# A two-layer graph network on one core: last products tile by tile, nine buffers for adj, the branch's verdict earlier among the products, four blocks by parts

## The chip, the cores and the metric

One core of a Trainium2 chip runs the whole kernel. A core has TensorE (PE, matrix products, with a queue of its own, PEld, for loading weights), VectorE (DVE), ScalarE (ACT), GpSimd (POOL) and SyncE (SP), each with an instruction queue that is worked through in order, 16 DMA engines, on-chip memory and PSUM, in which TensorE accumulates. SP, ACT and POOL issue the DMAs here. The metric is the device time of one execution in microseconds; less is better.

## The reference, cut to what matters

x is 4096 x 512 and adj 4096 x 4096, both float32. adj is nonzero in under one per cent of its entries (two random draws of 1/256, made symmetric, and the diagonal).

```python
def layer0(inp, adj, W, b):
    rowsum = adj.sum(axis=1)
    d = where(rowsum > 0, rowsum ** -0.5, 0.0)
    return relu(((d[:, None] * adj * d[None, :]) @ inp) @ W + b)

def layer1(inp, adj, W, a, wtrans):
    h = inp @ W
    e = leaky_relu(h @ a[:512] + (h @ a[512:]).T, 0.2)
    att = softmax(where(adj > 0, e, -1e12), axis=1)
    neg = -softmax(where(adj > 0, -e, -1e12), axis=1)
    return elu(concatenate([att @ inp, neg @ inp], axis=1) @ wtrans)

h = relu(layernorm(x));  x = x + layer0(h, adj, ...)
h = relu(layernorm(x));  x = x + layer1(h, adj, ...)
```

## The kernel before, in words

**Layer 0** is a dense product. It is computed as d * (adj @ y) + b with y = d * (relu(LN(x)) @ W), y staying on chip as 32 row blocks of 128 x 512. The 32 row blocks of the output are done in eight groups, `GROUPS`: (first block, count) = (26,6), (16,4), (20,4), (0,4), (4,4), (8,4), (12,4), (24,2). For a group, PSUM holds one accumulator of 128 x 512 for each of its blocks, and the inner loop runs over the 32 blocks j of y: a tile `at` of the transposed adj is loaded by SP (`load_at`, L794; two blocks j a tile in groups of four, four in the last group) and each accumulator gets one product a block (`multiply`, L804). A product of 128 x 512 float32 is two TensorE instructions.

*Group 0* (L817 to L859) also makes y. For each block j: POOL loads x (`load_x`, five buffers), DVE takes its statistics (L410), ACT normalizes it to hx (L633), PE transposes it (L645), DVE copies it, PE multiplies it by W (`project`, L676); SP loads the row block of adj in four pieces of 512 KB (`load_adj`, L657, pool `ain`, four buffers), three of them summed by ACT (L666) and one by DVE (L668), the sum becomes d (`scale`, L688 to L693), and ACT scales the projection to y (L699). Then six products follow with that block.

*Groups 1 to 7* are `group` (L907). It begins with `finish0` for the group before (L734): DVE takes all accumulators from PSUM (L741), then for each block POOL loads x, DVE adds it, takes the layer norm's statistics, ACT normalizes to h (L633), DVE makes the two scores of the attention (L757), and h with its score goes out as rows to eight tables in memory (`put_row`, L420): the table of the early pair by POOL, the seven others by ACT, or, for group 6, kept in a list `puts` and issued by SP at the end of group 7. Group 6's scores s reach other rows by `spread_s` (PE and ACT, through memory) and `load_s` (a broadcast load). DVE also packs each at tile into a byte mask (`pack`, L711, with flags at L715), which POOL stores into the tables' rows (L727). While groups 2, 3 and 4 run, the at tiles of groups 7, 6 and 5 are loaded once more, through the pool `early` with two buffers, and packed ahead of time (`EARLY`, L921). The pool `at` of groups 1 to 6 has five buffers.

*Lists.* From the flags DVE makes sorted lists of neighbours (`make_lists`, rounds at L375 and L377, spread over the steps of groups 3 to 6), which POOL turns into row indices (L390).

*The turn to layer 1.* A pair is two blocks of 64 rows. The pair 16 (blocks 33 and 32) is done early, inside and behind group 7: POOL gathers its rows of table 4 (`gather0`), DVE and ACT make the weights (`weights0`), PE multiplies (`product0`, L997) once group 7's products are done. `finish0` of blocks 24 and 25 follows, then `judge` (L880), which decides on DVE with one tiny product (`ok_ps`, L902) whether the lists hold everything: its `verdict` is read by all engines and chooses a branch, sparse or dense (L1181). Here it is sparse.

**Layer 1**, `sparse_layer1` (L1054), goes through the other 31 pairs from 17 on. A pair takes 22 gathers on POOL (8, 6 and 8 of 128 rows each, L428), in six tile slots, two pairs deep; the even block needs the first two parts, the odd block the last two. For a block: scores (L440), exponentials (L453), masks (L460), a tree of sums (L465 to L471) giving `total`, 14 products u (L1110), a column sum of total on PE (cs, L476) and its inverse (L478), us = u scaled (L1119), its transposes (tp, L486) and, for a pair, eight products with wtrans (o, L1133), elu and the output. The blocks in `first` (the first two) have exponentials part by part as gathers come, and their column sum behind the products u; the others have the column sum ahead of them. wtrans (`wt_sb`, 2 MB) is loaded by POOL behind the gathers of the first pair (L1156). In pairs 18 to 22, a copy on POOL (`mark`, L1078) waits for the last gather of its pair.

The scheduler may move instructions within an engine's queue unless `keep_in_program_order` pins one. A pool that opens gets memory that a closed one has left, and its first loads wait for the last users of that memory.

Of the kernel before, what the change touches and what calls it, by code (L numbers as in the profile page):

```python
# [19 lines left out]
P = 128  # L20
# [12 lines left out]
NE = 8  # L33
# [224 lines left out]
def gcn_gat_kernel(  # L258
# [97 lines left out]
    def rows_of(g, e):  # L356
        return table[g][e * ER : e * ER + EN, :].rearrange("(k p) c -> p k c", p=P)
# [21 lines left out]
    def table_rows(g, c, lst):  # L379

        li = list_pool.tile([P, CAPS[c]], I32, tag=f"li{c}", name=f"li{g}_{c}")
# [111 lines left out]
    with sbuf(name="y0", bufs=1) as y_pool, sbuf(name="wa", bufs=1) as wa_pool, sbuf(name="bits", bufs=2) as bits_pool, sbuf(name="small0", bufs=4) as small, ExitStack() as lists:  # L493
# [14 lines left out]
        )  # L508
        dummy = list_pool.tile([P, sum(CAPS)], F32, tag="lst", name="dummy")
        dummy = dummy[:, : NH * STR // P].bitcast(I32)  # L510
        nc.gpsimd.memset(dummy, EN)
        for g in range(2):
            nc.gpsimd.dma_start(
                out=lst_dram[g].rearrange("(p n) o -> p (n o)", p=P), in_=dummy
            )
        flags = [list_pool.tile([P, EJ * NE, 2 * NH], F32, name=f"flags{g}") for g in range(2)]
# [3 lines left out]
        wa_bc = [wa_pool.tile([P, F], F32, tag=f"wa{g}", name=f"wa{g}") for g in range(2)]  # L520
        zero = list_pool.tile([P, 3 * EN], F32, tag="keys", name="zero")
        zero = zero[:, :ROW].bitcast(I32)
        nc.gpsimd.memset(zero, 0)
        for g in range(NTAB):
            nc.gpsimd.dma_start(
                out=table[g].rearrange("(e r) c -> e r c", r=ER)[:, EN, :], in_=zero[:NE]
            )

        nc.gpsimd.dma_start(
            out=rows_of(tab0, late0 // EJ)[:, late0 % EJ : late0 % EJ + n_late, :],  # L530
            in_=zero.unsqueeze(1).to_broadcast([P, n_late, ROW]),
        )
        y_tiles = {}
# [5 lines left out]
        def make_keys(g):  # L539


            bits = list_pool.tile([P, 2, EJ * NE, NH], BF16, tag="flag16", name=f"flag16_{g}")
# [11 lines left out]
            keys[g] = list_pool.tile([P, 3, EN], F32, tag="keys", name=f"keys{g}")  # L554
            lst[g] = list_pool.tile([P, sum(CAPS)], F32, tag="lst", name=f"lst{g}")
# [6 lines left out]
            one = list_pool.tile([P, EN], F32, tag="one", name=f"one{g}")  # L562
            for c in range(3):
                nc.vector.tensor_scalar(one, key[:, c], 0.0, None, ALU.is_gt)
                nc.vector.tensor_reduce(cnt[:, c : c + 1], one, AX.X, ALU.add)

        def make_places(g):
# [3 lines left out]
            for e in range(NE + 1):  # L571
                nc.tensor.matmul(o_ps[:, e, 0:3], before[:, e, :], cnt, start=True, stop=True)
            o = list_pool.tile([NH, NE, 3], F32, tag="o", name=f"o{g}")
            tot = list_pool.tile([NH, 4], F32, tag="tot", name=f"tot{g}")
            nc.vector.tensor_copy(tot[:, 0:3], o_ps[:, NE, 0:3])
            begin = list_pool.tile([NH, 3], F32, tag="begin", name=f"begin{g}")
            nc.vector.memset(begin[:, 0:1], 0.0)
# [156 lines left out]
        def finish0(work, i0, acc, last=False):  # L734

            to_last = (i0, len(acc)) == GROUPS[-2]
            ys = []
            n_y = 4 if (i0, len(acc)) in GROUPS[-2:] else 6
            for j, a in enumerate(acc, i0):
                y = work.tile([P, F], F32, tag="y", name=f"y{j}", bufs=n_y)  # L740
                nc.vector.scalar_tensor_tensor(  # L741
                    y, a, d_all[:, j : j + 1], b_bc, ALU.mult, ALU.add
                )
                ys.append(y)
            for j, y in enumerate(ys, i0):
                xt = work.tile([P, F], F32, tag="xr", name=f"xr{j}")
# [36 lines left out]
        def load_s(queue, i0, n):  # L783

            j = i0
            while j < i0 + n:
                k = min(i0 + n, j - j % 4 + 4) - j
                queue.dma_start(
                    out=s_bc[j // 4][:, j % 4 * P : (j % 4 + k) * P],
                    in_=s_dram[j * P : (j + k) * P].partition_broadcast(P),  # L790
                )
                j += k

        def load_at(pool, i0, n, j0, nj):  # L794
# [8 lines left out]

        def multiply(acc, j0, at, between=None):  # L804
            for c in range(at.shape[1]):
                for it, a in enumerate(acc):
                    if between and it == len(acc) // 2:
                        between()
                    nc.tensor.matmul(  # L809
                        a,  # L810
                        at[:, c, it * P : (it + 1) * P],
                        y0[j0 + c],
                        start=j0 + c == 0,
                        stop=j0 + c == NJ - 1,
                    )

        i0, n = GROUPS[0]  # L817
        with sbuf(name="w0", bufs=1) as w0_pool, sbuf(name="at6", bufs=5) as at_pool, sbuf(name="ain", bufs=4) as ain, sbuf(name="ln", bufs=3) as ln_pool:
            w0_sb = w0_pool.tile([P, FC, F], F32, name="w0_sb")
# [60 lines left out]
        def judge():  # L880
# [20 lines left out]
            ok_ps = bank("ok_ps")  # L901
            nc.tensor.matmul(ok_ps[0:1, 0:1], all_ok, ones[:, 0:1], start=True, stop=True)  # L902
            verdict = const.tile([1, 1], I32, name="verdict")
# [3 lines left out]
        def group(b, work, at_pool, early, step):  # L907

            nonlocal pending
            i0, n = GROUPS[b]  # L910
            nj = 8 // n
            for jp in range(NJ // 2):
                if jp == 0:
                    finish0(work, *pending)
                    acc = [bank(f"acc{i0 + k}") for k in range(n)]
                if 2 * jp % nj == 0:
                    at = load_at(at_pool, i0, n, 2 * jp, nj)
                    multiply(acc, 2 * jp, at)
                if (i0, n) not in EARLY:
# [4 lines left out]
                if jp == 8:  # L924
                    spread_s(pending[0], len(pending[1]))
                if jp == 12:
                    load_s(nc.scalar, pending[0], len(pending[1]))
                step(jp)
            pending = (i0, acc)

        late = ctx.enter_context(sbuf(name="late", bufs=1, side="right"))
        late_h = late.tile([P, n_late, ROW_W], F32, name="late_h")
        late_m = late.tile([P, EJ, TT * P], U8, name="late_m")
        ut0 = late.tile([P, 2, FC, P], F32, name="ut0")

        with sbuf(name="work0", bufs=2) as work, sbuf(name="at", bufs=5) as at_pool, sbuf(name="early", bufs=2) as early:
            for b in range(1, len(GROUPS) - 1):
# [14 lines left out]
        with sbuf(name="work2", bufs=2) as work, sbuf(name="at2", bufs=5) as at_pool, sbuf(name="scratch", bufs=1) as scratch, sbuf(name="pair", bufs=1) as pair:  # L952
# [39 lines left out]

            def product0(r):
                u0[r] = bank(f"u{r}")
                for gt, k0, n in parts0(r):
                    for k in range(n):
                        nc.tensor.matmul(  # L997
                            u0[r],
# [3 lines left out]
                            stop=False,  # L1002
                        )

            def late_product0(r):
# [13 lines left out]
            def step(jp):  # L1019
# [4 lines left out]
                if jp == 10:  # L1024
                    gather0(0)
                    weights0(blocks[0])
                if jp == NP - 1:
                    for put in puts:
                        tc.keep_in_program_order(put())
# [24 lines left out]
    def sparse_layer1():  # L1054
        with ExitStack() as pools:
# [167 lines left out]
```

## Time and profile before

| | us |
|---|---|
| median of three runs | 2175.85 (2171.43 to 2177.98) |
| the profiled execution | 2161.19 |
| its span in the profile | 2159.4 |

The profiled execution is 0.7% below the median. Its page also gives, of engines and memory:

| engine or queue | what it does | busy or moved |
|---|---|---|
| PE acc<-y,at (L809) | products of groups 0 to 7 | 898.7 us |
| PE u<-g,p (L1110) | products of layer 1 | 764.7 us |
| POOL g<-table,idx (L428) | 704 gathers | 745.1 us, 1058 ns each |
| DMA | 523.86 MB moved | 243 GB/s over the span |

How to read it: busy time counts an engine's instructions, with pipelined matmuls run together; "idle before, with a releaser" is the time for which the engine stood still ahead of an instruction, and what let it go on. PEclk is the clock granted to TensorE as a share of full speed, 0.986 in this execution. SPq, POOLq and ACTq are the DMA queues. Group 0 ends at 340.8 us, group 6 at about 1028, group 7 at about 1084, and the branch is decided at 1098.6.

### The profile page before, as it was taken

What the parts mean: (1) busy time and instruction counts of PE and PEld (TensorE: products, weight loads), DVE (VectorE), ACT (ScalarE), POOL (GpSimd) and SP (SyncE); (2) the same over time, 40 slices, a digit from 0 to 9 for tenths busy, and PEclk for the clock granted to TensorE, in tenths of its full rate; (3) what the DMA queues carried; (4) which work ended last, traced back from release to release, by engine and by line L of the source; (5) the groups of instructions that cost most, each with busy time, mean ns of one, the idle gap of its engine ahead of it and who ended that gap; (6) DMA issues with size and microseconds to landing.
All of it is one profiled execution on the core that took longest, in us unless ns stands there. A gap on an engine that the chain in (4) does not pass through costs nothing.

```text
span 2159.4 us, 16968 instructions
## 1 busy us (share of the span) xinstructions
PE 2076.2 (96%) x5208; PEld 940.4 (44%) x5208; DVE 1038.8 (48%) x2427; ACT 407.8 (19%) x760; POOL 939.5 (44%) x1018
## 2 busy tenths in 40 slices
PE   7898999999999799999987999999999999999998
PEld 3344443444444344444433444444444444444443
DVE  5444414242489637920454454555454454444451
ACT  5555520000000000000121111212221212212111
POOL 2010002121212330140557667777777777777740
PEclk9999999999999999999998999999999999999999
DMA  9898927777785967274888888888888888888850
GB/s 362 321 328 317 356 81 268 245 232 265 239 279 182 342 184 261 85 244 128 297 255 287 243 243 253 258 258 255 260 251 242 241 244 241 242 243 242 242 169 21
DMA packets 185915, 523.86 MB, mean 243 GB/s; under 512 B 25683, under 2 KB 34995, under 8 KB 185814
## 3 DMA queue, kind: packets, MB, share of 16 engines
q0 software_dynamic: 74384, 285.71, 43.2%
q1 hardware_dynamic: 80544, 180.84, 24.3%
q10 hardware_dynamic: 30886, 56.14, 7.3%
q8 instruction: 42, 0.69, 0.1%
q14 instruction: 59, 0.48, 0.1%
HBM read 419.67 MB, written 102.92 MB: 242 GB/s over the span
## 4 chain that ended last, share of the span: by engine, by line
PE 69%; DMA 15%; DVE 6%; issue 5%; POOL 3%; ACT 1%; ACTq 0%; SPq 0%; POOLq 0%; DVEq 0%
PE u L1110 31%; PE acc L809 24%; PE o L1133 10%; DMA table<-h 4%; DMA at<-in_adj_t 4%; POOL g L428 3%; DMA ar<-in_adj 3%; DMA xt<-in_x 2%; PE yp L676 2%; PE tp L486 1%; DMA g<-table,idx 1%; DVE m L711 1%; DVE lst L375 1%; DVE keys L377 1%; ACT ar L666 1%
## 5 line engine op out<-in xcount | busy, mean ns | idle before, releaser
L809 PE MATMUL acc<-y,at 128*128 128x512 f32 x2048 | 898.7, 596 | 16.0 <-DMA at<-in_adj_t 16.0
L428 POOL DMA_INDIRECT g<-table,idx x704 | 745.1, 1058 | 256.5 <-issue 187.4
L1110 PE MATMUL u<-g,p 128*128 128x512 f32 x1736 | 764.7, 598 | 3.1 <-DVE p L460 3.1
L809 PEld LDWEIGHTS acc<-y,at 128*128 128x128 f32 x2048 | 388.1, 191 | 493.4 <-issue 469.7
L1110 PEld LDWEIGHTS u<-g,p 128*128 128x128 f32 x1736 | 327.4, 192 | 391.0 <-issue 369.9
L440 DVE TENSOR_TENSOR z<-g,s_bc 128x512 f32<-128x512 f32 (+1 forms) x128 | 79.8, 624 | 438.2 <-DMA g<-table,idx 419.5
L1133 PE MATMUL o<-wt_sb,ut 128*128 128x512 f32 x512 | 225.1, 593 | 0.5 <-ACT ut L490 0.5
L453 ACT ACTIVATE p<-z 128x896 f32<-128x896 f32 (+1 forms) x132 | 115.5, 924 | 373.1 <-DVE z L449 326.4
L460 DVE SCALAR_TENSOR_TENSOR p<-g,p 128x384 f32<-128x384 uint8 (+1 forms) x256 | 143.0, 619 | 65.0 <-ACT p L453 63.0
L711 DVE TENSOR_SCALAR m<-at 128x1024 uint8<-128x1024 f32 (+2 forms) x142 | 88.2, 631 | 167.3 <-DMA at<-in_adj_t 151.2
L727 POOL DMA_DIRECT2D table<-m x71 | 55.5, 784 | 230.1 <-DVE m L711 187.4
L676 PE MATMUL yp<-w_sb,hx_t 128*128 128x512 f32 x256 | 126.2, 640 | 22.9 <-ACT y L699 21.1
L1133 PEld LDWEIGHTS o<-wt_sb,ut 128*128 128x128 f32 x512 | 94.9, 190 | 107.7 <-issue 106.8
L666 ACT ACTIVATE ar<-ar 128x1024 f32<-128x1024 f32 x96 | 100.6, 1049 | 50.4 <-DMA ar<-in_adj 48.4
L1119 ACT ACTIVATE us<-u,rl 128x512 f32<-128x512 f32 x62 | 42.4, 684 | 356.6 <-issue 182.0
L390 POOL DMA_INDIRECT ld<-li,off x48 | 44.2, 921 | 145.4 <-DMA ld<-li,off 91.7
L676 PEld LDWEIGHTS yp<-w_sb,hx_t 128*128 128x128 f32 x256 | 51.9, 206 | 92.3 <-issue 62.0
L637 POOL DMA_DIRECT2D xt<-in_x x28 | 16.0, 570 | 169.8 <-ACT hx L633 144.1
L629 ACT ACTIVATE rrb<-rrb 128x1 f32<-128x1 f32 x32 | 5.4, 193 | 396.7 <-DVE rrb L628 313.6
L375 DVE MAX8 lst<-keys 128x8 f32<-128x512 f32 x120 | 79.3, 680 | 0.8
L377 DVE MATCH_REPLACE8 keys<-lst,keys 128x512 f32<-128x512 f32 x114 | 76.2, 671 | 0.0
L757 DVE SCALAR_TENSOR_TENSOR prod<-h,wa 128x512 f32<-128x512 f32 x60 | 41.2, 687 | 63.4 <-ACT h L633 27.0
(150 smaller groups left out, 1080.5 us busy)
## 6 DMA issues: line engine op xcount, KB each, us to landing
at<-in_adj_t SPq DMA_DIRECT2D x136, 512.0 KB, 5.3
ar<-in_adj SPq DMA_DIRECT2D x128, 512.0 KB, 6.6
table<-h ACTq DMA_DIRECT2D x182, 258.0 KB, 6.0
table<-m POOLq DMA_DIRECT2D x55, 256.0 KB, 6.3
at<-in_adj_t SPq DMA_DIRECT2D x32, 384.0 KB, 9.8
g<-table,idx POOLq DMA_INDIRECT x704, 4.3
xr<-in_x POOLq DMA_DIRECT2D x32, 256.0 KB, 4.7
x1d<-y POOLq DMA_DIRECT2D x32, 256.0 KB, 3.9
```

Source lines behind the costliest of these rows:

```text
L375: nc.vector.max(top, keys[:, c, :])
L377: nc.vector.match_replace(keys[:, c, :], top, keys[:, c, :], 0.0)
L428: nc.gpsimd.indirect_dma_start(out=gt[:, k, :], out_offset=None, in_=table[2 * n // RPT], in_offset=bass.IndirectOffsetOnAxis(ap=idx[n // ...
L440: return nc.vector.tensor_tensor(z, t.to_broadcast([P, n, RB]), s_bc[r // 8][:, r % 8 * RB : (r % 8 + 1) * RB].unsqueeze(1).to_broadcast([ ...
L453: nc.scalar.activation(p[:, :, g, :], z, AF.Exp, scale=(1.0, -1.0)[g])
L460: nc.vector.scalar_tensor_tensor(e, m, 0.0, e, ALU.is_gt, ALU.mult)
L666: i = nc.scalar.activation(ar, ar, AF.Identity, accum_out=part[:, c : c + 1])
L676: nc.tensor.matmul(yp, hx_t[j][:, c * P : (c + 1) * P], w0_sb[:, c, :], start=c == 0, stop=c == FC - 1,)
L711: i = nc.vector.tensor_scalar(m, at, 0.0, None, ALU.is_gt)
L809: nc.tensor.matmul(a, at[:, c, it * P : (it + 1) * P], y0[j0 + c], start=j0 + c == 0, stop=j0 + c == NJ - 1,)
L1110: nc.tensor.matmul(u, p[:, k0 + k].rearrange("p g c -> p (g c)"), gt[:, k, :F].bitcast(F32), start=k0 + k == 0, stop=k0 + k == nk - 1,)
L1133: nc.tensor.matmul(po, ut[:, g, c, :], wt_sb[:, g * FC + c, :], start=g == 0 and c == 0, stop=g == 1 and c == FC - 1,)
```

## The change

- In groups 1 to 7 the products of the last two at tiles are kept back (`ends`) and done at the end, accumulator by accumulator. `finish0` of groups 6 and 7 evicts and finishes block by block instead of evicting all first.
- The pool `ain` has nine buffers instead of four, and the pool `at` of groups 1 to 6 nine instead of five. To make room, the lists' working tiles move to a pool `make` opened after group 0, and two constant tiles (dummy, zero), whose stores fill parts of memory at the start, take two buffers of `ain`.
- `product0` of block 33 is split: nine products, `finish0` and `judge` with `ok_ps`, then five products, all in this order.
- Group 6's `load_s` moves from ACT (step 12 of group 7) to SP, right ahead of the 28 puts.
- `first` holds four blocks: 36 and 37 too are done by parts, with the column sum behind the products.
- wt_sb is loaded by SP's queue instead of POOL's.

```diff
@@ finish0
-            ys = []
-            for j, a in enumerate(acc, i0):
+            def evict(j):
                 y = work.tile([P, F], F32, tag="y", name=f"y{j}", bufs=n_y)
                 nc.vector.scalar_tensor_tensor(
-                    y, a, d_all[:, j : j + 1], b_bc, ALU.mult, ALU.add
-                )
-                ys.append(y)
-            for j, y in enumerate(ys, i0):
+                    y, acc[j - i0], d_all[:, j : j + 1], b_bc, ALU.mult, ALU.add
+                )
+                return y
+            by_tile = last or to_last
+            ys = {} if by_tile else {j: evict(j) for j in range(i0, i0 + len(acc))}
+            for j in range(i0, i0 + len(acc)):
+                y = evict(j) if by_tile else ys[j]
@@ group 0
-        with ... sbuf(name="ain", bufs=4) as ain, ...:
+        with ... sbuf(name="ain", bufs=9) as ain, ...:
+            dummy = ain.tile([P, RC], F32, tag="ain", name="dummy")
...
+            zero = ain.tile([P, RC], F32, tag="ain", name="zero")
...
@@ judge
-            nc.tensor.matmul(ok_ps[0:1, 0:1], all_ok, ones[:, 0:1], start=True, stop=True)
+            tc.keep_in_program_order(
+                nc.tensor.matmul(ok_ps[0:1, 0:1], all_ok, ones[:, 0:1], start=True, stop=True)
+            )
@@ group
+            ends = []
...
-                    multiply(acc, 2 * jp, at)
+                    if 2 * jp < NJ - 2 * nj:
+                        multiply(acc, 2 * jp, at)
+                    else:
+                        ends.append((2 * jp, at))
...
-                if jp == 12:
+                if jp == 12 and early:
                     load_s(nc.scalar, pending[0], len(pending[1]))
                 step(jp)
+            for a in acc:
+                for j0, at in ends:
+                    multiply([a], j0, at, at0=acc.index(a))
             pending = (i0, acc)
+        make_pool = lists.enter_context(sbuf(name="make", bufs=1))
...
-        with ... sbuf(name="at", bufs=5) as at_pool, sbuf(name="early", bufs=2) as early:
+        with ... sbuf(name="at", bufs=9) as at_pool, sbuf(name="early", bufs=2) as early:
@@ the turn to layer 1
-            def product0(r):
-                u0[r] = bank(f"u{r}")
+            def product0(r, lo=0, hi=n_block):
+                if lo == 0:
+                    u0[r] = bank(f"u{r}")
                 for gt, k0, n in parts0(r):
-                    for k in range(n):
-                        nc.tensor.matmul(
+                    for k in range(max(lo - k0, 0), min(hi - k0, n)):
+                        i = nc.tensor.matmul(
...
+                        if r == blocks[0]:
+                            tc.keep_in_program_order(i)
...
                 if jp == NP - 1:
+                    tc.keep_in_program_order(load_s(nc.sync, pending[0], len(pending[1])))
                     for put in puts:
                         tc.keep_in_program_order(put())
...
-            product0(blocks[0])
+            product0(blocks[0], hi=n_block - 5)
             finish0(work, *pending, last=True)
             verdict = judge()
+            product0(blocks[0], lo=n_block - 5)
@@ sparse_layer1
-            first = order[:2]
+            first = order[:4]
...
-                nc.gpsimd.dma_start(out=wt_sb, in_=wtrans.rearrange("(c p) f -> p c f", p=P))
+                nc.sync.dma_start(out=wt_sb, in_=wtrans.rearrange("(c p) f -> p c f", p=P))
```

More of the change, by code (lines that the diff above doesn't have):

```diff
@@ L379, in table_rows @@
     def table_rows(g, c, lst):
-        li = list_pool.tile([P, CAPS[c]], I32, tag=f"li{c}", name=f"li{g}_{c}")
+        li = make_pool.tile([P, CAPS[c]], I32, tag=f"li{c}", name=f"li{g}_{c}")
         src = lst[:, LOFF[c] : LOFF[c] + CAPS[c]]
@@ L508, in gcn_gat_kernel @@
         )
[L509 to L514, printed above, removed]
-            )
         flags = [list_pool.tile([P, EJ * NE, 2 * NH], F32, name=f"flags{g}") for g in range(2)]
@@ L520, in gcn_gat_kernel @@
         wa_bc = [wa_pool.tile([P, F], F32, tag=f"wa{g}", name=f"wa{g}") for g in range(2)]
[L521 to L532, printed above, removed]
         y_tiles = {}
@@ L539, in make_keys @@
         def make_keys(g):
-            bits = list_pool.tile([P, 2, EJ * NE, NH], BF16, tag="flag16", name=f"flag16_{g}")
+            bits = make_pool.tile([P, 2, EJ * NE, NH], BF16, tag="flag16", name=f"flag16_{g}")
             kp = []
@@ L553, in make_keys @@
                 kp.append(k2)
-            keys[g] = list_pool.tile([P, 3, EN], F32, tag="keys", name=f"keys{g}")
-            lst[g] = list_pool.tile([P, sum(CAPS)], F32, tag="lst", name=f"lst{g}")
+            keys[g] = make_pool.tile([P, 3, EN], F32, tag="keys", name=f"keys{g}")
+            lst[g] = make_pool.tile([P, sum(CAPS)], F32, tag="lst", name=f"lst{g}")
             key, cnt = keys[g], count[:, g]
@@ L561, in make_keys @@
                 nc.vector.tensor_tensor(key[:, 2 * a], key[:, 2 * a], key[:, 1], ALU.subtract)
-            one = list_pool.tile([P, EN], F32, tag="one", name=f"one{g}")
+            one = make_pool.tile([P, EN], F32, tag="one", name=f"one{g}")
             for c in range(3):
@@ L572, in make_places @@
                 nc.tensor.matmul(o_ps[:, e, 0:3], before[:, e, :], cnt, start=True, stop=True)
-            o = list_pool.tile([NH, NE, 3], F32, tag="o", name=f"o{g}")
-            tot = list_pool.tile([NH, 4], F32, tag="tot", name=f"tot{g}")
+            o = make_pool.tile([NH, NE, 3], F32, tag="o", name=f"o{g}")
+            tot = make_pool.tile([NH, 4], F32, tag="tot", name=f"tot{g}")
             nc.vector.tensor_copy(tot[:, 0:3], o_ps[:, NE, 0:3])
-            begin = list_pool.tile([NH, 3], F32, tag="begin", name=f"begin{g}")
+            begin = make_pool.tile([NH, 3], F32, tag="begin", name=f"begin{g}")
             nc.vector.memset(begin[:, 0:1], 0.0)
@@ L787, in load_s @@
                 k = min(i0 + n, j - j % 4 + 4) - j
-                queue.dma_start(
+                i = queue.dma_start(
                     out=s_bc[j // 4][:, j % 4 * P : (j % 4 + k) * P],
@@ L792, in load_s @@
                 j += k
+            return i
         def load_at(pool, i0, n, j0, nj):
@@ L802, in load_at, with multiply @@
             return at
-        def multiply(acc, j0, at, between=None):
+        def multiply(acc, j0, at, between=None, at0=0):
             for c in range(at.shape[1]):
-                for it, a in enumerate(acc):
+                for it, a in enumerate(acc, at0):
                     if between and it == len(acc) // 2:
@@ L817, in gcn_gat_kernel @@
         i0, n = GROUPS[0]
-        with sbuf(name="w0", bufs=1) as w0_pool, sbuf(name="at6", bufs=5) as at_pool, sbuf(name="ain", bufs=4) as ain, sbuf(name="ln", bufs=3) as ln_pool:
+        with sbuf(name="w0", bufs=1) as w0_pool, sbuf(name="at6", bufs=5) as at_pool, sbuf(name="ain", bufs=9) as ain, sbuf(name="ln", bufs=3) as ln_pool:
+            dummy = ain.tile([P, RC], F32, tag="ain", name="dummy")
+            dummy = dummy[:, : NH * STR // P].bitcast(I32)
+            nc.gpsimd.memset(dummy, EN)
+            for g in range(2):
+                nc.gpsimd.dma_start(
+                    out=lst_dram[g].rearrange("(p n) o -> p (n o)", p=P), in_=dummy
+                )
+            zero = ain.tile([P, RC], F32, tag="ain", name="zero")
+            zero = zero[:, :ROW].bitcast(I32)
+            nc.gpsimd.memset(zero, 0)
+            for g in range(NTAB):
+                nc.gpsimd.dma_start(
+                    out=table[g].rearrange("(e r) c -> e r c", r=ER)[:, EN, :], in_=zero[:NE]
+                )
+            nc.gpsimd.dma_start(
+                out=rows_of(tab0, late0 // EJ)[:, late0 % EJ : late0 % EJ + n_late, :],
+                in_=zero.unsqueeze(1).to_broadcast([P, n_late, ROW]),
+            )
             w0_sb = w0_pool.tile([P, FC, F], F32, name="w0_sb")
@@ L901, in judge @@
             ok_ps = bank("ok_ps")
-            nc.tensor.matmul(ok_ps[0:1, 0:1], all_ok, ones[:, 0:1], start=True, stop=True)
+            tc.keep_in_program_order(
+                nc.tensor.matmul(ok_ps[0:1, 0:1], all_ok, ones[:, 0:1], start=True, stop=True)
+            )
             verdict = const.tile([1, 1], I32, name="verdict")
@@ L934, in gcn_gat_kernel @@
         ut0 = late.tile([P, 2, FC, P], F32, name="ut0")
-        with sbuf(name="work0", bufs=2) as work, sbuf(name="at", bufs=5) as at_pool, sbuf(name="early", bufs=2) as early:
+        with sbuf(name="work0", bufs=2) as work, sbuf(name="at", bufs=9) as at_pool, sbuf(name="early", bufs=2) as early:
             for b in range(1, len(GROUPS) - 1):
```

## The prediction

> **What bounds the kernel now.** I read the head of the page first, then TensorE's list of waits, then a table by stages, and last the places of the longest waits.
>
> ```profile
> span 2159.4 us, 16968 instructions
> PE 2076.2 (96%) x5208; PEld 940.4 (44%) x5208; DVE 1038.8 (48%) x2427; ACT 407.8 (19%) x760; POOL 939.5 (44%) x1018
> ```
>
> TensorE (PE) is busy for 96% of the span, so what a scheduling change can win is the 83.2 us (2159.4 − 2076.2) in which it is not, and a few us of low clock. The list of its waits says who owes them:
>
> ```profile
> PE yp L676 <- ACT y L699: 21.1, 6, 6.6
> PE acc L809 <- DMA at<-in_adj_t: 16.0, 5, 4.8
> PE cs L476 <- DVE total L471: 15.3, 2, 13.7
> ```
>
> Six waits of the projection for y, five of the adjacency products for their loads, and one of 13.7 us for the column sums. The table by stages (columns: stretch, length, busy time of PE, PEld, DVE, ACT, POOL with instructions, granted clock, DMA share, GB/s) says where:
>
> ```profile
> 0.00:345.00 345.00, 307.54 (x779) 139.15 (x779) 144.57 (x466) 159.26 (x323) 40.87 (x79) 0.96 0.79 282
> 345.00:550.00 205.00, 205.00 (x474) 90.39 (x475) 76.86 (x213) 10.01 (x22) 35.46 (x61) 0.99 0.78 263
> 550.00:720.00 170.00, 170.00 (x421) 75.44 (x420) 135.82 (x345) 6.20 (x15) 42.14 (x59) 1.00 0.73 246
> 720.00:800.00 80.00, 68.14 (x151) 28.97 (x150) 33.43 (x74) 1.88 (x3) 24.52 (x32) 0.96 0.79 265
> 800.00:1084.00 284.00, 284.00 (x689) 125.63 (x688) 141.49 (x371) 16.37 (x32) 67.71 (x98) 1.00 0.61 205
> 1084.00:1162.00 78.00, 57.71 (x147) 26.53 (x146) 39.02 (x99) 16.90 (x34) 48.77 (x50) 0.89 0.84 275
> 1162.00:1340.00 178.00, 171.97 (x440) 78.56 (x439) 82.36 (x150) 34.49 (x57) 126.71 (x122) 0.99 0.81 246
> ```
>
> TensorE's gaps are four: 37.5 us in group 0 (345 − 307.54), 11.9 us at 720 to 800, 20.3 us at 1084 to 1162 (the last group's end and the first blocks of layer 1), 6.0 us until 1340. Elsewhere PE is full. The clock column adds to it: after a long gap the next four or five matmuls start 0.85 us apart instead of 0.43, so a gap of 4 us or more costs about 2 us on top.
>
> **Part 1, the seam of groups 0 and 1 (ain and at buffers).** The timeline of PE there:
>
> ```profile
> 333.72 7.03 PE L809 MATMUL acc<-y,at 128*128 128x512 f32 x16
> 344.89 2.93 PE L809 MATMUL acc<-y,at 128*128 128x512 f32 x3 [4.14 <-DMA at<-in_adj_t]
> ```
>
> Group 1's first load goes into memory that group 0's last tile of adj_t held, so it is issued at 340.8, with the last product, and lands 4.1 us later. In the changed order that memory belongs to row-sum tiles, which ScalarE has done with by about 300: the load goes out 40 us earlier. What goes is 4.14 us and five starts of 0.42 us too many, and a further half instruction: **−6.6** (at least the bare 4.1).
>
> **Part 2, group 0's row sums.** TensorE needs six products, a projection and four transposes a row block: (12 + 8) × 0.43 + 4 × 0.11 = 9.0 us. Its stalls are for y; y waits for the row sum in ScalarE, whose queue and SP's show (0 to 345 us for the first, the whole span for the second):
>
> ```profile
> ACT ar L666 <- DMA ar<-in_adj: 48.4, 37, 2.8
> SPq L657 <- ACT ar L666: 117.0, 61, 7.2
> ```
>
> SP can't issue a load until one of four buffers is free (61 waits, 117 us), and ScalarE then waits for what lands: a loop of issue, 6.6 us of transfer, 1.05 us of sum. Nine buffers cut it. But there is a second loop, which the change leaves: ScalarE's normalization frees the x buffer, GpSimd loads the next x, and VectorE's statistics of it stand ahead of the next row sum's scale:
>
> ```profile
> DVE sta L410 <- DMA xt<-in_x: 85.2, 24, 6.8
> ```
>
> From block 12 to block 26 the normalization advances 10.5 us a block ((250.8 − 103.2) / 14), 1.5 us slower than PE could. The 48.4 us of row-sum waits, over 32 blocks, are 1.5 us a block: if all of them lay on this loop it would fall to PE's 9.0, and the group would be shorter by 24 to 27 us, its whole stall but the start. If none does, nothing changes. In the step that I followed, y leaves ScalarE at 247.5, directly behind a row sum that had waited 1.67 us for its load. I take half, **−12**, and keep −25 and +3 (the deeper ring delays something else) as ends. DMA is at 0.87 to 0.96 of its engines in the first 240 us, moving 2.65 MB a block, 7.8 us at 340 GB/s, under PE's 9.0: a limit near, but not reached.
>
> At the start five adj_t loads of 384 KB now go out on SP ahead of the first row-sum tiles (in the order of the changed kernel), some 2 MB, 5.8 us at 340 GB/s, of which most lies beside the x and weight loads that the first y also needs (first product at 23.4 us): **+1.5** (0 to 3).
>
> **Part 3, groups 2 to 4.** VectorE is busy 135.8 of 170 us there (packing masks of two streams and making lists), SP waits for it, and the lead of the loads, 27 us at 541, is used up by 720. Then PE starves: 2.22, 4.82, 3.87 and 0.96 us, 11.9 in all, and three slow starts, 16 us. Nine buffers let the packing of the ordinary stream run four loads further ahead, in the order up to 13.7 us (two loads of a group of four tiles, 16 products of 0.86 us); the early stream keeps its two buffers, and SP's order of the two is nearly unchanged, so the lockstep stays and only the stock grows. 13.7 us of stock against 16 of stall; VectorE has room to catch up after 800 (half busy). **−13**; ends −4 (only the first waits go) and −16.
>
> **Part 4, last group to layer 1.** Four edits meet. (a) Deferred and done tile by tile, the last 16 products of group 6 end its first tile 12 products (10.3 us) before its last, and the eviction goes tile by tile too: the early pair's gathers start some 7 us earlier. (b) The scores of block 32 no longer hold VectorE until 1088, so the last evictions start about 4.5 us earlier, and with them the verdict (now 1098.6, 14.4 us after the last product); the five products that follow the verdict (4.3 us) cover what is left of PE's wait of 2.23. (c) wt_sb leaves GpSimd's queue: its 0.96 + 0.30 us of issue and the 0.69 that a gather waited for it, 2.0 us. (d) Blocks 36 and 37 by parts: the sum of block 36 no longer stands ahead of its products, which need only the first of two gathers. This is PE's longest wait:
>
> ```profile
> 1146.89 0.63 PE L486 MATMUL tp<-ident,us 128*128 128x128 f32 x4
> 1161.22 0.56 PE L476 MATMUL cs<-ones,total 128*128 128x1 f32 x2 [13.70 <-DVE total L471]
> ```
>
> At that place 13.7 + 1.8 us go. But GpSimd issues gathers end to end there, 22 a pair at 1.25 to 1.35 us, and it, not PE, sets the pace until 1331; all that PE wins beyond GpSimd's own gain it waits for a pair or two later (it waits 6.0 us there already). GpSimd's gain: 4.5 of verdict, 2.0 of wt_sb, and one of its marks, which by the changed order stands two gathers later and so out of reach of a landing:
>
> ```profile
> 1228.38 0.18 POOL L1078 COPY mark<-g 128x1 int32<-128x1 int32 x1 [4.89 <-DMA g<-table,idx]
> ```
>
> That is 4 us. 10.5 us in all; I take **−9**, since the puts, held on SP behind the new load of s_bc, now move their 7.2 MB beside the last evictions. Ends −2 and −15.
>
> The Trainium skill, page "DMA: Bandwidth & Descriptors", section "Issuing engines are not separate DMA queues", speaks against (c): moving a transfer to another engine saves only its issue. By it the term would be 1.3 us instead of 2.0.
>
> **The sum.** −6.6 − 12 + 1.5 − 13 − 9 = −39 against the profiled execution of 2161.2 us (span 2159.4 and 1.8 around it): 2122. The median of the runs, 2175.85, lies 0.68% above that execution; so 2122 × 1.0068 = **2137 us**.
>
> **The rivals.** *The loops stay* (24%): the x loop alone sets group 0 (−3), the early stream's two buffers alone set groups 2 to 4 (−4), GpSimd's gathers take back all but 3 us of part 4. −6.6 − 3 + 1.5 − 4 − 3 = −15: 2146, with the median's scale 2161. For it: the 85.2 us row, and that VectorE is 80% busy. Against it: SP's 117 us of waiting for row-sum buffers. *All of it* (11%): −6.6 − 25 − 16 − 15 = −63, 2098, as a median 2113. *Slower* (10%): nine row-sum buffers let SP keep twice as many loads in flight, and the x loads queue behind them. Each us that an x load takes longer is a us a block on the x loop, for 24 blocks (the 24 waits of its row). The other terms are −27 and the ring's gain at most −1.5 a block; so it decides from 6.3 + 1.5 + 27 / 24 = 8.9 us an x load. Were x loads served in order behind 2 MB more, at 340 GB/s, they would take 5.9 us longer; at a bit over half of that, 3.5, it is 24 × 2 − 27 = +21, 2182, as a median 2197. For it: a DMA share near 0.95. Against it: the two x loads issued after 240, at a share of 0.69, take 5.2 and 5.8 us, those before, at 0.87 to 0.96, 6.3 in the mean, hardly more. *Nothing moves* (5%): what one place wins another gives back, 2176.
>
> The same page, section "Queues, rings and completion order", says that each DMA engine goes round the queues that have work, a packet at a time; x is on GpSimd's queue, so by it a deeper ring on SP costs x nothing, and the slower rival has no price. No run here shows it yet; the x rows above agree as far as they go.
>
> **How the numbers follow.** My forecast has 50%, with a range of its own of 2122 to 2152 (group 0 from none to all but a few us). The range that should hold 8 in 10 takes in the first two rivals down to 2108 and up to 2167, and leaves out the slower one, nothing moves, and a sliver of the best. Within 0.3% (6.5 us) is about what a measurement of this kernel can tell from no change; faster than that 0.85, same 0.05, slower 0.10.
>
> **What would show it.** Right: group 1's first product follows group 0's last without a gap; "SPq ar <- ACT ar" falls far under 117 us; PE waits under 4 us at 720 to 800; no wait of 13.7 us for total36, but some us of waits for tp or u in the next three pairs; verdict about 10 us after group 7's last product. Wrong: x loads of 9 us or more; the stall of 720 moved to 780 or later at its old size; verdict no earlier.

## The result, and the profile after

The changed kernel takes 2152.11 us in the median of four runs (2144.26 to 2154.16), beside 2176.91 (2171.43 to 2179.23) of the kernel before: 0.9883 of it, 95% interval 0.9852 to 0.9914, some 25 us less. I had said 2137, range 2108 to 2167. Its profiled execution took 2154.16 us, span 2152.4, which is only 7 under the profiled execution of before (2159.4). So one profile says 7 and the times say 25; where the other 18 are is the first thing to find out.

The list of TensorE's waits in the changed kernel:

```profile
PE tp L486 <- issue: 18.1, 1, 18.1
PE yp L657 <- ACT y L680: 17.9, 7, 5.3
PE u L1131 <- DVE p L460: 12.1, 1, 12.1
...
PE ok_ps L908 <- DVE all_ok L905: 6.2, 1, 6.2
```

The waits for adj loads (16.0) and for the column sums (15.3) are gone, those for y are nearly as before (17.9, before 21.1), and three new or longer ones stand there: 18.1 ahead of transposes, 12.1 ahead of products, 6.2 (2.2 before) for the verdict. By two of the same stretches (same columns):

```profile
720.00:800.00 80.00, 80.00 (x189) 35.17 (x188) 33.01 (x76) 2.29 (x5) 25.45 (x32) 1.00 0.76 248
...
1084.00:1162.00 78.00, 47.84 (x121) 22.23 (x121) 27.36 (x54) 13.23 (x27) 55.94 (x57) 0.80 0.87 275
```

TensorE is full from 720 to 800: the stall at 720 is gone and did not come back later. The stretch 1084 to 1162 is worse than before: 30 us without work (before 20), at a clock of 0.80.

Because the stretches shift against each other, I compare by landmarks, read from the timelines: the end of group 0, the last product of group 7 (called E7), and behind it the verdict, the first gather of layer 1, the starts of blocks 34 and 36, and the end.

| kernel (one profile each) | group 0 ends | E7 | verdict | first gather | block 34 | block 36 | end |
|---|---|---|---|---|---|---|---|
| before | 340.6 | 1083.8 | +14.8 | +16.3 | +36.3 | +77.8 | +1075.6 |
| before, once more | 337.7 | 1081.8 | +14.9 | +16.5 | +48.8 | +90.2 | +1088.3 |
| changed | 337.5 | 1057.7 | +14.4 | +18.3 | +68.7 | +95.6 | +1094.7 |
| changed, once more | 333.9 | 1054.1 | +16.5 | +19.0 | +69.8 | +96.9 | +1085.6 |

Layer 0 ends 24 to 30 us earlier in every pairing. What is lost is lost between E7 and block 36.

### The profile page after: what moved, and what is told of

The parts are those of the page before. It is cut to its first block, busy times and chain, and to the rows that moved or that the text cites. A ratio compares the mean times of both kernels' runs of the same rounds, so it can differ in the third digit from the quotient of the medians.

```text
span 2152.4 us, 17006 instructions
## 1 busy us (share of the span) xinstructions
PE 2071.5 (96%) x5208; PEld 938.0 (44%) x5208; DVE 1040.5 (48%) x2429; ACT 409.4 (19%) x764; POOL 945.2 (44%) x1017
## 4 chain that ended last, share of the span: by engine, by line
PE 85%; DMA 5%; issue 4%; DVE 2%; ACT 1%; POOL 1%; another core or an unknown queue 1%; DVEq 0%; POOLq 0%; ACTq 0%
PE u L1131 35%; PE acc L795 35%; PE o L1154 10%; DMA xt<-in_x 4%; PE yp L657 2%; PE tp L486 1%; PE u L1014 1%; DVE sta L410 0%; ACT ar L647 0%; DMA ar<-in_adj 0%; PE cs L476 0%; POOL g L428 0%; DMA ld<-dummy 0%; DMA g<-table,idx 0%
## 5 line engine op out<-in xcount | busy, mean ns | idle before, releaser
L1131 PE MATMUL u<-g,p 128*128 128x512 f32 x1736 | 767.2, 599 | 16.8 <-DVE p L460 12.1
L453 ACT ACTIVATE p<-z 128x896 f32<-128x896 f32 (+2 forms) x136 | 116.0, 903 | 203.2 <-issue 114.6
L657 PE MATMUL yp<-w_sb,hx_t 128*128 128x512 f32 x256 | 123.4, 628 | 19.9 <-ACT y L680 17.9
L390 POOL DMA_INDIRECT ld<-li,off x48 | 45.2, 942 | 160.0 <-DMA ld<-li,off 104.0
L647 ACT ACTIVATE ar<-ar 128x1024 f32<-128x1024 f32 x96 | 100.1, 1043 | 17.9 <-DMA ar<-in_adj 17.9
L449 DVE SCALAR_TENSOR_TENSOR z<-z 128x896 f32<-128x896 f32 (+2 forms) x68 | 70.8, 1041 | 2.2
```

The costliest lines, as they stand in the source:

```text
L453: nc.scalar.activation(p[:, :, g, :], z, AF.Exp, scale=(1.0, -1.0)[g])
L647: i = nc.scalar.activation(ar, ar, AF.Identity, accum_out=part[:, c : c + 1])
L657: nc.tensor.matmul(yp, hx_t[j][:, c * P : (c + 1) * P], w0_sb[:, c, :], start=c == 0, stop=c == FC - 1,)
L1131: nc.tensor.matmul(u, p[:, k0 + k].rearrange("p g c -> p (g c)"), gt[:, k, :F].bitcast(F32), start=k0 + k == 0, stop=k0 + k == nk - 1,)
```

## The experiments

**Both kernels once more.** No edit.

> The kernel before, unchanged, once more. The profiled execution of before (2161.2 us) lies 15 us under its median (2175.9). Theory A (TensorE's signals that arrive 9 to 17 us late at the turn to layer 1 in the changed kernel, at 1095 to 1123 us, are made by the change): a second profile of before shows no such wait, and its span is again near 2160 while its times stay near 2176. Theory B (late signals at the turn come with most executions of either kernel, and the profiled execution of before was one without them): the second profile has a span near 2170 to 2177, with some 10 to 16 us of waits for transposes or sums around 1110 to 1130 that the first one lacks, and group 7's last product again at 1084.

> The changed kernel, unchanged, once more. Both theories: layer 0 ends near 1057 us (group 7's last product), 27 us before that of the kernel before. Theory A: the late signals at 1095 to 1123 are there again, about 25 us in sum, and the time is near 2152. Theory B: they differ from one execution to the next, so this profile's waits between 1090 and 1130 differ by more than 5 us from the first one's, while layer 0 agrees within 1 us.

Measured: before 2175.79 us (10 runs, ratio to before 0.9995, 0.9977 to 1.0014), changed 2149.68 (ratio 0.9879, 0.9833 to 0.9924). The second profile of before has a span of 2170.1, 10.7 more than the first, and the table says where: layer 0 is even 2 us shorter, and 12.4 us are lost between E7 and block 36. The timeline of ScalarE, first profile of before, then second:

```profile
1114.98 0.65 ACT L490 COPY ut<-tp 128x256 f32<-128x256 f32 x2 [1.12 <-PE tp L486]
...
1117.00 0.65 ACT L490 COPY ut<-tp 128x256 f32<-128x256 f32 x2 [0.74 <-PE tp L486]
```

```profile
1116.41 0.65 ACT L490 COPY ut<-tp 128x256 f32<-128x256 f32 x2 [2.65 <-PE cs L476]
...
1127.60 0.65 ACT L490 COPY ut<-tp 128x256 f32<-128x256 f32 x2 [7.95 <-remote]
```

In the first, ScalarE copies each transposed block 0.03 to 0.04 us after TensorE's last transpose of it ended. In the second the last copy comes 6.8 us after its transposes (they ended at 1120.8), with nothing of the profile to release it ("remote"). I call that a late signal. The changed kernel's first profile has the same in larger pieces, on VectorE and TensorE:

```profile
1112.02 0.17 DVE L478 RECIPROCAL rl<-cs 128x1 f32<-128x1 f32 x1 [18.95 <-remote]
```

```profile
1094.77 0.28 PE L476 MATMUL cs<-ones,total 128*128 128x1 f32 x2
1113.16 1.12 PE L486 MATMUL tp<-ident,us 128*128 128x128 f32 x4 [18.11 <-issue]
1126.33 2.05 PE L1131 MATMUL u<-g,p 128*128 128x512 f32 x2 [12.05 <-DVE p L460]
```

The column sum ended at 1095.05; VectorE took it at 1112.02, 17 us later, and TensorE stood still for 18.1. Theory B holds as far as that before has late signals too, and that its first profile was an execution without them. Its second half fails: I said the waits of the changed kernel would differ between two profiles by over 5 us, and they are 17.4 and 12.0 in the second against 18.1 and 12.1. In both profiles they are larger than in before's second, which has 4.7 and 9.8 at the same places.

**Blocks 36 and 37 whole again; only the buffers.**

```diff
-            first = order[:4]
+            first = order[:2]
```

> The changed kernel with blocks 36 and 37 whole again (first = order[:2]). My prediction's reason (GpSimd's gathers set the pace until about 1331, so the long wait at block 36 only moves): time within 3 us of the changed kernel's. Rival (the wait at block 36 was paid in full and is now gone for good): 12 to 15 us slower than the changed kernel, near 2165.

Measured: 2154.43 us, 0.9898 (0.985 to 0.9946), 5 us over the changed kernel of the same session. That is less than the 12 to 15 of the rival, but the two intervals are too wide to exclude it. In its profile the wait at block 36 is 5.2 us, not 13.7. One reason may be that the late signals ahead of it gave the gathers time; but in before's second profile the wait at block 36 is still 13.8 us with late signals ahead of it, so this stays open. Where the signals are on time the edit was not tried.

The second takes back the four parts behind layer 0 as well: `first` to two, wt_sb to GpSimd, the deferral and the split (their edits are below).

> The changed kernel with the four other parts undone, so that only the nine buffers in both parts of layer 0 (with the moved list tiles) and the eviction tile by tile with the moved load of s_bc are left. By the changed kernel's profile the buffers win 6.6 at the seam of groups 0 and 1, 16 at 720 to 800 and 3 in group 0. If the turn to layer 1 costs what it cost before, the time is 25 us under before, near 2151, the same as the whole change: then the other parts bring nothing. If the other parts bring what my prediction said (9), it is near 2160.

Measured: 2155.19 us, 0.9886 (0.9811 to 0.9962), against 0.9879 of the whole change. Without the four other parts the kernel is as fast as with them, as far as these intervals tell; that is not far, since its four runs go from 2140 to 2170 us, and the two expectations lie 9 us apart.

**wt_sb on GpSimd again; no split; no deferral.**

```diff
-                nc.sync.dma_start(out=wt_sb, in_=wtrans.rearrange("(c p) f -> p c f", p=P))
+                nc.gpsimd.dma_start(out=wt_sb, in_=wtrans.rearrange("(c p) f -> p c f", p=P))
```

```diff
-            product0(blocks[0], hi=n_block - 5)
+            product0(blocks[0])
...
-            product0(blocks[0], lo=n_block - 5)
```

```diff
-                    if 2 * jp < NJ - 2 * nj:
+                    if True:
```

> The changed kernel with wt_sb loaded by GpSimd again. Theory 1 (at the turn TensorE's signals come late because SP, with wt_sb, waits all the while for the same TensorE signal as ScalarE and VectorE): the waits of 17.6 and 12.3 us ahead of blocks 32's transposes and 34's products fall to under 6 and the time drops by 10 or more. Theory 2 (they come late whenever the gathers have run for some 20 us and TensorE runs dry, whoever waits): both waits stay within 4 us of their size; then wt_sb on GpSimd costs only its 1.3 to 2 us of gather issue, and the time is within 4 us of the changed kernel's 2150.

> The changed kernel with the product of block 33 in one piece again, ahead of the verdict. The five products put behind the verdict were to cover TensorE's wait for it; in the changed kernel's profiles that wait is 6.3 and 8.4 us, where the kernel before had 2.2 and 2.5. If the split only opened the wait it meant to fill, the wait here is 2 to 4 us, block 32 starts 4 us earlier after the verdict, and block 34 does not start later; time within 4 us of 2150, since behind the verdict gathers and late signals bind. If the split helps, the verdict itself comes 3 us later or more without it.

> The changed kernel without the deferral of the last products of a group. My prediction's step: the deferral brings the early pair's gathers forward by some 7 us and the verdict by part of 4.5. If so, the verdict comes 3 us or more later after group 7's last product than in the changed kernel (14.4 and 16.5 us). Rival, from the profiles: with the deferral VectorE finishes block 24 wholly before it takes block 25 from PSUM, and the two chains of 6 us stand in line; without it they overlap, and the verdict is 13.5 to 14.5 us after the last product, no later than with it. Time within 4 us of 2150 by the rival, 3 to 7 slower by my step.

Measured, all in one session on one chip: 2152.93 us, 0.9885 (0.9868 to 0.9901); 2150.62, 0.988 (0.9858 to 0.9902); 2153.54, 0.9871 (0.9842 to 0.9899). None can be told from the changed kernel, which has 0.9883 and 0.9879 in other sessions; a part worth less than some 8 us would not show. With wt_sb on GpSimd the two waits do fall (to 4.9 and 4.4 for the transposes and 3.3 for block 34), as theory 1 wanted, but a third of the same kind appears 30 us later, ahead of block 36:

```profile
1105.37 14.67 PE L1131 MATMUL u<-g,p 128*128 128x512 f32 x28 [3.25 <-DVE p L460]
...
1142.49 2.90 PE L1131 MATMUL u<-g,p 128*128 128x512 f32 x3 [9.60 <-issue]
```

So SP's wait with wt_sb is not the cause: late signals come without it too, here and in the kernel with the buffers alone, which also loads wt_sb by GpSimd. Without the split the wait for the verdict is 4.0 us instead of 6.2 and 8.3, and the time is the same. Without the deferral the verdict comes 17.1 us after E7, against 14.4 and 16.5: less than my step's 3 us against the later of the two, and not the rival's 14 either. The kernel with the buffers alone has no deferral either, and there the verdict comes at +13.9, where the rival wanted it. What the rival said of the deferral is to be seen on VectorE, in the changed kernel first, then in the one without the deferral:

```profile
1058.66 0.74 DVE L722 SCALAR_TENSOR_TENSOR y<-acc,d_all,b_bc 128x512 f32<-128x512 f32 x1
...
1064.80 0.74 DVE L722 SCALAR_TENSOR_TENSOR y<-acc,d_all,b_bc 128x512 f32<-128x512 f32 x1
```

```profile
1063.74 0.75 DVE L722 SCALAR_TENSOR_TENSOR y<-acc,d_all,b_bc 128x512 f32<-128x512 f32 x1
...
1065.13 0.74 DVE L722 SCALAR_TENSOR_TENSOR y<-acc,d_all,b_bc 128x512 f32<-128x512 f32 x1
```

In the changed kernel block 24 leaves PSUM 1.0 us after E7 (before: 4.4), but block 25 only when block 24's whole chain of 6.1 us is through, at +7.1 (before: +5.8, the two chains interleaved). Without the deferral the two follow 1.4 us apart, as in before. From the first of them to the verdict it is 13.4 us with the deferral and 10.4 without (10.4 in the kernel with the buffers alone as well, 10.4 in before). So standing in line costs 3 us, and the early start is given back. That the verdict is late all the same in the run without the deferral (+17.1) comes from its first eviction, at +6.8: VectorE was still at the early pair's weights, which it could begin 1.4 us ahead of E7, when their rows had landed; in the changed kernel it was 5.8 and 3.7 us.

**Four ain buffers.**

```diff
-        with ... sbuf(name="ain", bufs=9) as ain, ...:
+        with ... sbuf(name="ain", bufs=4) as ain, ...:
```

> The changed kernel with four buffers for group 0's adj (at keeps nine). My prediction's part 2 takes half of group 0's stall from the ring of four (12 us); the profiles of the changed kernel show group 0 ending at 337.5 and 333.9, of the kernel before at 340.6 and 337.7, some 3 us. By my part 2 group 0 ends 8 us later or more than in the changed kernel; by what the profiles show (the x loop is left and sets the pace) 2 to 5 us later, at 338 to 341, and SP again waits over 100 us for ScalarE's sums. The seam to group 1 stays closed if only the at buffers' place matters, and opens again by 4 us if it is the row-sum tiles' place.

Measured: 2168.33 us, 0.9944 (0.9926 to 0.9963), 0.6% or 13 us over the changed kernel's ratios. Group 0 ends at 347.0, 9.5 and 13 us later than in the two profiles of the changed kernel. (This end differs from profile to profile: in the ten whose group 0 is the changed kernel's it lies between 329 and 337.5, at 334 in the mean.) SP's and ScalarE's waits in group 0, with four buffers and then with nine:

```profile
SPq L638 <- ACT ar L647: 110.5, 59, 7.0
```

```profile
ACT ar L647 <- DMA ar<-in_adj: 70.1, 41, 5.3
```

```profile
SPq L638 <- ACT ar L647: 26.3, 19, 6.6
```

```profile
ACT ar L647 <- DMA ar<-in_adj: 17.9, 10, 4.8
```

The ring was a loop that counted: 13 us against the mean of ten, and my 12 us for it hold. The seam to group 1 stays closed with four buffers.

**The first loads in the old order; five at buffers; direct loads.** The first pins SP's loads of group 0's first six blocks:

```diff
-                nc.sync.dma_start(
+                i = nc.sync.dma_start(
                     out=ar, in_=adj[j * P : (j + 1) * P, c * RC : (c + 1) * RC]
                 )
+                if j < 6:
+                    tc.keep_in_program_order(i)
```

and the same for `load_at` where it loads group 0's tiles of the first six blocks.

> The changed kernel with SP's loads of group 0's first six blocks pinned in the order of the program, so that the first row-sum tiles go ahead of the five adj_t tiles, as they did before the change. Group 0 with four buffers ended at 347.0 in the changed kernel and at 340.6 and 337.7 in the kernel before: some 8 us of the ring's gain are lost elsewhere in the group. If the new order at the start is the cause, the first product starts at about 23.4 instead of 25.6, TensorE's loss in the first 60 us falls from 17.8 to 14 and group 0 ends 4 to 8 us earlier, near 327; time some 4 to 8 under 2150, faster than both kernels. Rival (the x loop sets the pace, and the start is absorbed by it): group 0 ends within 3 us of the changed kernel's 329 to 337.

Measured: 2125.29 us (five runs, 2121.34 to 2128.68), 0.9812 of before, 0.9799 to 0.9826. It beats before; against the changed kernel, which was timed in other sessions, part of the difference is the session's, since the late signals that cost that kernel time are missing in this one. Group 0 ends at 324.9, and E7 is 1045.1; the two kernels with direct loads below, whose layer 0 is the changed kernel's, were profiled in the same session and have 333.8 and 334.3, 1054.0 and 1054.4. Against these two the pinned order brings 9 us of layer 0, against the shortest of the ten group 0s (329.2) 4; from the end of group 0 to E7 it is 720 us in all of them that have nine at buffers. By that the changed kernel would have taken some 2134 us beside the 2165.8 of before, 0.985 of before (an estimate from the 9 us). My reason for it fails: the first product starts at 25.9, no earlier than in the changed kernel (25.6 and 26.4; before 23.4), and in the first 60 us TensorE is idle for 16.4 us (changed 15.6, before 11.9). Two things that I had not looked at stand in the way there. The row sum of block 0 is put together on VectorE, behind a copy that waits for TensorE; first this run, then before:

```profile
23.46 0.69 DVE L632 COPY hx_t<-tx 128x512 f32<-128x512 f32 x1 [6.19 <-PE tx L626]
24.07 0.14 DVE L671 TENSOR_REDUCE rs<-part 128x1 f32<-128x4 f32 x1
```

```profile
15.79 0.14 DVE L688 TENSOR_REDUCE rs<-part 128x1 f32<-128x4 f32 x1
```

And the two constant tiles that now take two of the nine buffers hold SP up until their stores are done, in the changed kernel (8.6 and 3.6 in this run, nothing of the kind in before):

```profile
SPq L638 <- DMA ld<-dummy: 7.7, 1, 7.7
...
SPq L638 <- DMA table<-zero: 4.6, 1, 4.6
```

There SP issues no row-sum load from 13.0 to 21.5 us. No run undoes either, so what they cost is not shown. The gain of the pinned order comes later. Its TensorE waits:

```profile
PE yp L659 <- ACT y L682: 11.0, 3, 6.3
PE cs L476 <- DVE total L471: 7.1, 3, 2.9
```

Three waits for y instead of seven, none after 120 us; from block 12 to 26 the normalization advances 9.5 us a block, in the changed kernel 10.4 and 10.1 (9.7 to 10.4 in the ten). Why an order of the first six blocks quickens the x loop 100 us later is open.

```diff
-        with ... sbuf(name="at", bufs=9) as at_pool, ...:
+        with ... sbuf(name="at", bufs=5) as at_pool, ...:
```

> The changed kernel with five at buffers in groups 1 to 6 (ain keeps nine). My prediction's part 3: the stall of 16 us at 720 to 800 comes back (13 at least), and the time is 13 to 16 over the changed kernel's 2150. The seam of groups 0 and 1 tells whose memory closed it: if the row-sum tiles lie under the first at tiles it stays closed, if not it opens by 4 us. Rival: without the stall in layer 0 the turn binds (its late signals and gathers), and of 16 us more in layer 0 less than half shows in the time.

Measured: 2166.59 us, 1.0001 (0.9988 to 1.0014): with five at buffers the whole change is worth nothing beside the before of the same session (2165.8). TensorE, from the timeline:

```profile
663.74 35.04 PE L795 MATMUL acc<-y,at 128*128 128x512 f32 x76 [6.46 <-DMA at<-in_adj_t]
...
739.38 0.84 PE L795 MATMUL acc<-y,at 128*128 128x512 f32 x1 [4.59 <-DMA at<-in_adj_t]
```

The stalls (6.46, 3.83, 2.68, 4.59) begin 64 us earlier than before and with another at 970 (5.86) they cost 33 us with the slow starts, twice the 16 of the kernel before; E7 is 1090.3, 6.5 later than before. The deferral holds two of the five tiles to a group's end, which leaves three for the lead: that would explain it, but five buffers without the deferral were not run. So my 16 us were too few by half. The rival can't be judged, because the late signals that it needs did not come in this run: here what layer 0 loses shows in full (against the pinned order E7 is 45.2 later and the span 43.9 longer). Its seam to group 1 is closed too.

The direct loads, for every pair but the early one, first by SP and then by GpSimd:

```diff
         for k in range(CHUNKS[a]):
+            if n != PAIR0:
+                nc.sync.dma_start(
+                    out=gt[:, k, :], in_=table[2 * n // RPT][k * P : (k + 1) * P, :]
+                )
+                continue
             nc.gpsimd.indirect_dma_start(
```

> The changed kernel, but the gathers of layer 1 are direct loads on SP of the same number of rows of the same tables, at fixed places: the rows that belong to each block are not looked up, so layer 1's result is left out. What it tells is where the late signals come from: in all profiles but the first one of before, ScalarE and VectorE start 4 to 33 us after the TensorE product that they wait for has ended, some 5 to 22 times in layer 1. If GpSimd's indirect loads (their queue, or what they report) are the cause, there is no such wait over 1 us here. If it is the 228 GB/s of rows that come in, or the branch, as many are left.

> The same with the direct loads issued by GpSimd, again at fixed places, layer 1's result left out. If the late signals come with GpSimd's queue, whatever the kind of load, they are there as in the changed kernel (5 or more over 1 us). If they come with the look-up of row numbers alone, there are none.

Measured, one run each: 2116.61 and 2116.67 us, no late signal. That says nothing on the cause, because start_ar and at5, which gather as ever, have none in that same session, and before takes 2165.8 in it instead of 2175 to 2181. Late signals came with the session here; whether the gathers' form has a part in them was not told.

## Why the prediction held, and where it did not

The measured 2152.1 lies in my range of 2108 to 2167, but 15 us above the 2137, at the upper end of the forecast's own 2122 to 2152. The direction and two of the four parts were right; that the sum still hit with the two others wrong is owed to the width of the range.

By landmarks. Of the clean profiles (without late signals) E7, and from E7 to the end, can be told apart: before 1083.8 and +1075.6; start_ar 1045.1 and +1074.4; at5 1090.3 and +1073.1. The turn and layer 1 then gain 1 to 2.5 us by one profile each, all else is layer 0.

1. *The seam* (−6.6): right. Group 1's first product follows without a gap in every variant. The memory's owner was not settled: it closes with nine of either buffer.
2. *Group 0* (−12 for the ring, +1.5 at the start, −10.5 in all): its size was wrong by a term I had called harmless. The ring alone gives 9.5 to 13, from four buffers (347.0) to nine (337.5 and 333.9). But group 0 with four buffers and the rest of the change is 6 to 9 us longer than in the kernel before (340.6 and 337.7). Net it is −5 (334 in the mean of the ten profiles whose group 0 is the changed kernel's, from 329 to 337.5, against 339), and the pinned order brings 4 to 9 more. "+1.5 (0 to 3)" is the failed term: it measured 6 to 9 us with four buffers, and 5 of these are there in the first 60 us (TensorE idle for 17.4 us, before 11.9 and 12.5). I priced the moved loads alone, by the first product's delay. I left out the two constant tiles in the ring and the later row sum on VectorE, and what the order of the first loads does to the x loop. How the cost divides among these is open.
3. *Groups 2 to 4* (−13): right in sign and near in size, 16. The stock sufficed for the whole stall.
4. *The turn* (−9): failed. "The last evictions start about 4.5 us earlier, and with them the verdict": the first does start 1.3 to 3.4 earlier, but block 25's stands behind block 24's chain, and the verdict is at +14.4 to +16.5 (before +14.8), the first gather 1 to 3 us later. "Verdict no earlier" stood on my list of signs of being wrong, and for this part it came. "The five products that follow the verdict (4.3 us) cover what is left of PE's wait": they were taken from ahead of the wait, which grew from 2.2 to 6.2 and 8.3. What wt_sb brings can't be told from nothing (0.9885 without it); the mark was not tried alone. In clean profiles block 36 starts 7 us earlier (+70.3 and +70.9, before +77.8), and by the end 1 to 2.5 us are left of it; start_ar has 7.1 us of waits for totals over the next pairs, which fits what I said of the gathers.
5. *The slower rival* is out: x loads issued after 60 us land in 5.7 us (start_ar) and 6.4 (at5), in before 6.4, while SP's waits for buffers fell from 117 us to 35 and 33 there (26 in the changed kernel). The rule of the Trainium skill that I set against it (page "DMA: Bandwidth & Descriptors", section "Queues, rings and completion order": each engine goes round its queues, packet by packet) agrees with these times; no run shows the rounds themselves.
6. *The scale*: I took the 0.68% between the first profile and the median for something spread over the span. It was 12 us of late signals between E7 and block 36, which that profile did not have. Where they occur, the changed kernel has more of them in that place (block 34 at +69 and +70 against +48.8), and from E7 to the end it takes 1094.7 and 1085.6 us there, before 1088.3: in such sessions the turn brings nothing in the mean, and the 25 us that the times show are layer 0's.

The sum by what was measured in clean profiles: −6.6 − 5 − 16 − 2 = −30, against my −39: 5.5 too much in group 0 and 7 in the turn, 3 too little in groups 2 to 4. Two readings of mine were off and change nothing: a block's loads in group 0 are 2.75 MB, 8.1 us at 340 GB/s (not 2.65 and 7.8), and the x loads before 240 us take 6.5 us in the mean (not 6.3).

## What to carry to other kernels

When work is put off to shorten a chain, look at what else stands on the engine at the end of it: an eviction that starts earlier wins nothing if the second one then waits for the first one's whole chain. A buffer that a deferral holds to the end is a buffer less for the lead, so size the two together (argued here, not shown). A tile lent to a ring of buffers holds up the loads behind it until its own use is over: 7.7 and 4.6 us of SP here. And profile the kernel before twice: the gap between one profiled execution and the median may sit in one place, and that place may be the one you change.

## What the runs showed of the hardware

I had not expected late signals: in 9 of 14 profiles ScalarE or VectorE takes up a column sum or a transposed block up to 33 us after TensorE had ended it (all after the first gathers of layer 1, free of other work meanwhile), and in the 5 others never over 1 us late. The largest, in the kernel with the buffers alone, kept TensorE from work for 40 us:

```profile
1166.60 0.56 PE L476 MATMUL cs<-ones,total 128*128 128x1 f32 x2 [40.65 <-DVE total L471]
```

In the profiles with late signals the trace also lacks semaphore records from layer 1 on (901 in the changed kernel's first, 1011 in before's second, 901 to 1011 in all nine, none in the clean ones), so the lateness may come from what records the events, or both from one thing. In the session in which all four profiles were clean, before took 2165.8 us, in the others 2175 to 2181. That session ran on another chip (15) than the two before it (7), and the chip of the first two profiles, one clean and one not, is not on record; so the chip, the session and the recording can't be told apart as causes. Which part of the machine delays the signals stays open: SP's wait with wt_sb is excluded (wt_pool and the kernel with the buffers alone), the gathers' form is not, since the runs that tried it had nothing to show.
